# Routing and row sends of a mixture-of-experts layer moved from the opening into the main loop, with edge decays in four matmuls

## The chip, the cores and the metric

The kernel runs on one core of one Trainium2 chip. The metric is the time of one execution in microseconds on the device. All data are 32-bit floats.

## The reference, cut to what matters

Two layers work on 4096 tokens (8 sequences of 512) of 256 features. Each normalises its input and adds two branches to it.

The first layer's branches are a bidirectional Mamba-2 mixer and a top-1 mixture of eight experts:

```python
zxbcdt = u @ in_proj_w.T                      # z, xBC, dt
dt = softplus(dt + dt_bias)                   # 8 heads, both directions
xBC = silu(causal_conv(xBC, conv_w) + conv_b) # 4 taps
A = -exp(A_log)
# per chunk of 128 tokens, a = A*dt, A_cs = cumsum(a) in the chunk
Y_diag = einsum(C, B, exp(segsum(a)), x*dt)
Y_off  = einsum(C, state, exp(A_cs))          # exp(A_cs): the "edge decay"
y = Y_diag + Y_off + x*D ; gate with silu(z), normalise, @ out_proj_w.T

probs = softmax(xt @ Wr + br); gate = max(probs); idx = argmax(probs)
h1 = relu(xt @ W1[idx] + b1[idx]);  y = (h1 @ W2[idx] + b2[idx]) * gate
```

The second layer's branches are latent attention with 16 heads and a top-2 mixture of seven experts with a fixed capacity. The change does not touch them.

## The kernel before, in words

**Opening.** For each of the 8 sequences the kernel normalises four tiles of 128 tokens (kept in `xn0`), transposes them on TensorE and projects them to 24 columns: 16 of `dt`, 8 of routing (`norm_and_project`, lines 143 and 148). Then `route()` computes on VectorE the softplus of `dt` (lines 372 to 386), the product `da` of `dt` and `A` (line 390), and the routing: softmax, first maximum, the rank of every token in its expert (two matmuls `both`, lines 204 and 205), the slot of every token in a list sorted by expert and padded to blocks of 128 (`slot0`, line 409), and the expert of every block (`w_idx`, line 418). It ends with 32 indirect DMAs issued by GpSimd, one per tile, that send the normalised rows to their slots in `xd0` (line 422). There are 39 blocks.

After `route()` comes the first sequence's projection and convolution (`x_part`, `skip`, `bc_part`), two `tokens` parts, and then:

- `decays()` makes sums of `da` within chunks, and their exponentials.
- `edges()` makes the edge decay of every token, head and direction: per sequence and direction four matmuls with 8 weight columns each (line 452), an exponential of 8 x 512 (line 457) into a tile `e8` of the tag `row`, and a DMA to `exd` in DRAM (line 458). Tiles of the tag `row` have eight buffers, which the convolution's `cv` and `th` and the token transposes' `xt` use too.

In this part the order of instructions on each engine is a planner's.

**Main loop.** 64 iterations, one per chunk (sequence, step, direction): iteration n issues the segment sums of chunk n+1 (`seg`, line 879), prepares chunk n+2 (`au` on GpSimd, line 864, and the broadcast load of edge decays `ex`, line 868), does the chunk's own products (`yd`, line 917; `yoff`, line 935; `sp`, line 943) and `weigh` of the next chunk (`mt`, line 911). Between these stand parts of the neighbouring sequences' projections (`others`). The order on every engine is as written (`tc.manual_schedule`).

Four times in each iteration, from iteration 2 on, `fill(1)` takes a piece from the generator `blocks()`, or, when that is at its end, from `late()`, which finishes sequences for the second layer. In the last eight iterations there are two more. `blocks()` has five pieces per block:

1. transposes of the block's rows (line 495), the copy `xdT` on ScalarE (line 497), and `fetch(j + 1)`: the rows of the next block by SyncE, its `w1`, `w2` and `b12` by three indirect DMAs of GpSimd (line 482)
2. and 3. the two halves of the first product (line 507), with the relu on ScalarE for the first half and on VectorE for the second
4. and 5. the two halves of the second product (line 520), the bias and the write to `yd0`.

The pool `e2` of the blocks is opened ahead of the loop in the place of `xn0` and of the routing's tiles, so its first loads wait for what still reads those.

Of the kernel before, what the change touches and what calls it, by code (L numbers as in the profile page):

```python
# [16 lines left out]
P = 128  # L17
# [3 lines left out]
TPB = S // P  # L21
# [35 lines left out]
def tile_kernel(ctx: ExitStack, tc: tile.TileContext, t, out: bass.AP):  # L57
# [48 lines left out]
    xtd = dram.tile([B, P, KC, S], FP, name="xtd", tag="xtd")  # L106
    exd = dram.tile([B, 2, NH, S], FP, name="exd", tag="exd")
    fdd = dram.tile([B, NH, S], FP, name="fdd", tag="fdd")
# [214 lines left out]
    dt = l0c.tile(D3, FP, name="dt", tag="dt")  # L323
    da = l0c.tile(D3, FP, name="da", tag="da")
    gate = ctile("gate", [P, NTILE])
# [5 lines left out]
    mid = l0c.tile([P, NTILE, NH], FP, name="mid", tag="mid")  # L331
    dec_all = l0c.tile(D3, FP, name="dec_all", tag="dec_all")

# [5 lines left out]

    def route():  # L340
        pool, big = r0p, r0b
        proj = big.tile([P, NTILE, 2 * NH + NE], FP, name="proj0", tag="proj0")
        xTs = {}
# [45 lines left out]
        V.tensor_scalar(ea, ea, -1.0, None, ALU.mult)  # L389
        V.tensor_tensor(da, dt, bc(ea, 1, D3), ALU.mult)  # L390


        _, pr = softmax_experts(big, proj[:, :, 2 * NH :], br)
        m, oh = first_max(big, pr, "a")
        V.tensor_copy(gate, m)
        rank, n = ranks(big, bank, oh, lambda shape: row("rk_b").rearrange("p (a b) -> p a b", a=2))
        over = big.tile([P, NE, NTILE], FP, name="over", tag="over")
# [5 lines left out]
        for e in range(1, NE):  # L403
            V.tensor_tensor(end[:, e : e + 1], end[:, e : e + 1], end[:, e - 1 : e], ALU.add)
        first = big.tile([P, NE], FP, name="first", tag="first")
        V.tensor_tensor(first, end, nb, ALU.subtract)
        V.tensor_scalar(first, first, float(P), None, ALU.mult)
        V.tensor_tensor(rank, rank, bc(first, 1, E3), ALU.add)
        V.tensor_copy(slot0, slots_of(big, oh, rank, "a"))


        B3 = [P, NBLK, NE - 1]
# [4 lines left out]
        V.tensor_scalar(be, be, float(P), pidx, ALU.mult, ALU.add)  # L417
        V.tensor_copy(w_idx, be)

        sent = []  # L420
        for i in range(NTILE):
            one = G.indirect_dma_start(
                out=xd0, out_offset=bass.IndirectOffsetOnAxis(ap=slot0[:, i : i + 1], axis=0),
                in_=xn[:, i, :], in_offset=None, bounds_check=NBLK * P - 1, oob_is_err=False,
            )
            for other in sent:
                tc.declare_no_dep(one.ins, other.ins, reason="rows go to slots of their own")
            sent.append(one)

    def decays():  # L430
        dp = bank("dp", [P, 2, NTILE * NH], 0)
        for d in range(2):
            T.matmul(
                dp[:, d, :].rearrange("p (t h) -> p t h", h=NH), LOW[d], da[:, :, d * NH : (d + 1) * NH],
                start=True, stop=True,
            )
        A.activation(dec_tok.rearrange("p d t h -> p d (t h)"), dp, AF.Exp)
        hs = bank("hs", [P, NTILE, NH], 1)
        for d in range(2):
            r = slice(d * HP2, (d + 1) * HP2)  # L440
            T.matmul(hs[r], LOW[d][r, r], da[r, :, d * NH : (d + 1) * NH], start=True, stop=True)
        V.tensor_copy(mid, hs)
        ta = bank("ta", [P, NTILE * 2 * NH], 0)
        T.matmul(ta, ones, da.rearrange(f2), start=True, stop=True)
        A.activation(dec_all.rearrange(f2), ta, AF.Exp)

    def edges():
        for b in range(B):
            for d in range(2):
                ct = bank("ct", [NH, S], 0)  # L450
                for c in range(TPB):
                    T.matmul(
                        ct[:, c * P : (c + 1) * P], da[:, b * TPB + c, d * NH : (d + 1) * NH], MSK[d],
                        start=True, stop=True,
                    )
                e8 = row("e8")
                A.activation(e8[:NH, :], ct, AF.Exp)
                Y.dma_start(out=exd[b, d], in_=e8[:NH, :])

    route()  # L460
    l1c = tl = w_r = rb = w_q = w_o = w_uk = w_uv = w_kv = band = slot1 = wsel = proj1 = vt0 = qk0 = r1b = noop = None
# [4 lines left out]
    with ExitStack() as es:  # L466
# [8 lines left out]

        def fetch(j):
            xd = e2.tile([P, DM], FP, name="xd", tag="xd", bufs=3)
            Y.dma_start(out=xd, in_=xd0[j * P : (j + 1) * P, :])
            got = [xd]
            for name, n, bufs in (("w1", KC * FF, 2), ("w2", FC * DM, 2), ("b12", FC + DM, 2)):  # L480
                w = e2.tile([P, n], FP, name=name, tag=name, bufs=bufs)
                G.indirect_dma_start(
                    out=w, out_offset=None, in_=t[name], bounds_check=NE * P - 1, oob_is_err=False,
                    in_offset=bass.IndirectOffsetOnAxis(ap=w_idx[:, j : j + 1], axis=0),
                )
                got.append(w)
            return got

        def blocks():
            got = fetch(0)  # L490
            for j in range(NBLK):
                xd, w1, w2, b12 = got
                tp = bank("xdT_ps", [P, DM], "e")
# [3 lines left out]
                A.copy(xdT, tp)  # L497
                if j + 1 < NBLK:
                    got = fetch(j + 1)
                yield  # L500
                hT = [e2.tile([P, FC // 2, P], FP, name="hT", tag="hT", bufs=2) for _ in range(2)]
                for half in range(2):
                    hp = bank("h_ps", [P, FC // 2, P], "e")
                    for i in range(FC // 2):
                        f = half * FC // 2 + i
                        for k in range(KC):
                            T.matmul(  # L507
                                hp[:, i, :], w1[:, k * FF + f * P : k * FF + (f + 1) * P],
                                xdT[:, k * P : (k + 1) * P], start=(k == 0), stop=(k == KC - 1),
                            )  # L510
                    for i in range(FC // 2):
                        f = half * FC // 2 + i
                        if half == 0:
                            A.activation(hT[half][:, i, :], hp[:, i, :], AF.Relu, bias=b12[:, f : f + 1])
                        else:
                            V.tensor_scalar(hT[half][:, i, :], hp[:, i, :], b12[:, f : f + 1], 0.0, ALU.add, ALU.max)
                    yield
                yp = bank("y_ps", [P, DM], "e")
                for f in range(FC):
                    T.matmul(  # L520
                        yp, hT[f // 4][:, f % 4, :], w2[:, f * DM : (f + 1) * DM], start=(f == 0), stop=(f == FC - 1)
                    )
                    if f == 3:
                        yield
                yo = e2.tile([P, DM], FP, name="yo", tag="yo")
# [325 lines left out]
        class Chunk:  # L851
# [9 lines left out]
            def prepare(self):  # L861
                d = self.d
                self.au = p1.tile(HH, FP, name="au", tag="au")
                G.tensor_tensor(self.au, bc(da[:, self.i, d * NH : (d + 1) * NH], 2, HH), bc(TRI[d], 1, HH), ALU.mult)  # L864
                if not self.first:
                    self.ex = p2.tile([P, HC, P], FP, name="ex", tag="ex", bufs=3)
                    for i in range(2):
                        Y.dma_start(
                            out=self.ex[HD * i : HD * (i + 1), :, :],
                            in_=bc(exd[self.b, d, i::2, self.cols], 0, [HD, HC, P]),  # L870
                        )
# [67 lines left out]
            def behind(self):  # L939
# [7 lines left out]
                else:  # L947
                    d = self.d
                    G.tensor_tensor(
                        heads(st), heads(st), bc(dec_all[:, self.i, d * NH : (d + 1) * NH], 2, HP), ALU.mult  # L950
                    )
# [39 lines left out]
        batch[1].load()  # L991
        r0.close()
        xs.close()
        e2 = es.enter_context(tc.tile_pool(name="e2", bufs=2, side="right"))

        with tc.manual_schedule(engines=ENGINES):
# [31 lines left out]

            rows, rest = blocks(), late()

# [5 lines left out]
            for n in range(N):  # L1036
# [6 lines left out]
                ahead = chunk[n + 1] if n + 1 < N else None  # L1043
                begun = n >= 2

# [8 lines left out]
                if n % 8 == 5 and next_:  # L1054
                    pending.append(beginning)
                if begun:
                    fill(1)
                if ahead:
# [4 lines left out]
                turn()  # L1063
                if begun:
                    fill(1)
                now.before()
                if ahead:
                    ahead.pairs(batch[ahead.b])
                if begun:
                    fill(1)  # L1070
                turn()
                now.behind()
                if ahead:
                    ahead.weigh()
                if begun:
                    fill(1)
                while work:
                    turn()
                if n >= N - 8:
                    fill(2)  # L1080
# [532 lines left out]
```

## Time and profile before

| | us |
|---|---|
| median of three runs | 2159.49 (2159.13 to 2172.04) |
| the profiled execution | 2153.93 |
| its span, first to last instruction | 2152.2 |
| TensorE busy | 1874.2 (87%) |
| VectorE busy | 1463.6 (68%) |
| ScalarE busy | 1187.6 (55%) |
| GpSimd busy | 636.4 (30%) |
| opening, to the first `yd` | 0 to 169.8 |
| first layer's main loop and its end | 169.8 to about 1121 |
| expert blocks in it | 182.7 to 907.2 |
| second layer | from there to the end |

The profile names the engines PE (TensorE), PEld (its weight loads), DVE (VectorE), ACT (ScalarE), POOL (GpSimd) and SP (SyncE); "L507" is line 507 of the kernel. A 32-bit matmul shows as two records, a transpose as one. Ends of matmuls are modelled, so consecutive records overlap a little: the spacing of starts tells more than the durations. The page's second part cuts the span in 40 slices of 53.8 us; each digit is a busy share in tenths, and PEclk is the clock granted to TensorE in tenths of full speed.

### The profile page before, as it was taken

How to read it: one execution, taken by the hardware profiler on the slowest of the kernel's cores; microseconds unless marked ns; L12 is line 12 of the kernel's file. 1: busy time of each engine (PE TensorE's matmuls, PEld its weight loads, DVE VectorE, ACT ScalarE, POOL GpSimd, SP SyncE). 2: the span in 40 equal slices, each digit the busy share in tenths (PEclk: the TensorE clock that was granted, in tenths of full speed). 3: DMA queues.
4: the chain of work that ended last, by engine and by line, in shares of the span. 5: the costliest groups of instructions: out<-in, count | busy, mean ns of one | idle time of the engine just before them, and what ended most of it. 6: DMA issues, size and time to landing. Idle time of an engine off the chain costs nothing. (4 is left out here: it accounts for less than half of the span.)

```text
span 2152.2 us, 33599 instructions
## 1 busy us (share of the span) xinstructions
PE 1874.2 (87%) x11792; PEld 1240.4 (58%) x11792; DVE 1463.6 (68%) x3328; ACT 1187.6 (55%) x2562; POOL 636.4 (30%) x592
## 2 busy tenths in 40 slices
PE   5649999999999999987867778999999999999785
PEld 5325666766766676644544444656666666666343
DVE  5745666767584666577648896766666676767795
ACT  2235453545444354545426676767677777777563
POOL 0075453646363454445410253000000000000452
PEclk9879999999999999988887788999999999999787
DMA  7134454646463464444523342121121212121354
GB/s 257 56 103 169 152 191 146 222 142 221 140 203 138 135 230 134 142 135 127 162 94 112 96 144 89 63 103 61 65 81 60 97 63 82 62 77 54 89 109 94
DMA packets 156361, 263.69 MB, mean 123 GB/s; under 512 B 25018, under 2 KB 112622, under 8 KB 144290
## 3 DMA queue, kind: packets, MB, share of 16 engines
q1 hardware_dynamic: 124544, 144.70, 21.2%
q0 software_dynamic: 22320, 107.55, 15.3%
q10 hardware_dynamic: 9330, 9.31, 1.3%
q8 instruction: 93, 1.52, 0.3%
q14 instruction: 74, 0.61, 0.1%
HBM read 193.44 MB, written 72.75 MB: 124 GB/s over the span
## 5 line engine op out<-in xcount | busy, mean ns | idle before, releaser
L1348 DVE TENSOR_SCALAR s<-s_ps 128x512 f32<-128x512 f32 x512 | 317.7, 683 | 235.8 <-PE s_ps L1343 185.9
L1358 ACT ACTIVATE s<-s,ng 128x512 f32<-128x512 f32 x512 | 354.2, 726 | 29.0 <-DVE ng L1354 22.2
L1365 PE MATMUL p_ps<-ident,s 128*128 128x128 f32 x2048 | 297.3, 289 | 71.0 <-ACT pT L1366 60.2
L1365 PEld LDWEIGHTS p_ps<-ident,s 128*128 128x128 f32 x2048 | 244.3, 147 | 155.9 <-ACT pT L1366 94.2
L1366 ACT COPY pT<-p_ps 128x512 f32<-128x512 f32 x512 | 278.9, 590 | 88.5 <-PE p_ps L1365 63.9
L1350 DVE CUSTOM_DVE_ANT_0 s<-s,band 128x512 f32<-128x512 f32 x512 | 322.5, 685 | 0.0
L1308 POOL DMA_INDIRECT yg<-yd,at x64 | 67.6, 1057 | 710.6 <-PE s_ps L1343 650.7
L688 PE MATMUL pj<-xT,w_in 128*128 128x512 f32 x384 | 197.5, 640 | 12.3 <-DVE cv L701 9.5
L1343 PE MATMUL s_ps<-kT,qT 16*128 16x512 f32 x1024 | 174.7, 698 | 17.5 <-DVE s L1348 10.9
L507 PEld LDWEIGHTS h_ps<-xdT,w 128*128 128x128 f32 x1248 | 153.9, 197 | 32.9 <-issue 19.0
L507 PE MATMUL h_ps<-xdT,w 128*128 128x128 f32 x1248 | 158.8, 282 | 10.3 <-ACT xdT L497 10.3
L864 POOL TENSOR_TENSOR au<-da,half 128x512 f32<-128x512 f32 x64 | 75.1, 1174 | 258.0 <-PE seg L879 162.4
L701 DVE SCALAR_TENSOR_TENSOR cv<-pj,w_conv_w,cv 128x511 f32<-128x511 f32 (+2 forms) x192 | 143.0, 746 | 9.8 <-issue 5.6
L520 PE MATMUL y_ps<-w,hT 128*128 128x256 f32 x624 | 148.2, 380 | 0.0
L1374 PE MATMUL o_ps<-pT,vt 128*32 128x256 f32 x2048 | 139.6, 415 | 0.0
L520 PEld LDWEIGHTS y_ps<-w,hT 128*128 128x128 f32 x624 | 115.9, 191 | 34.8 <-issue 19.4
L937 POOL TENSOR_TENSOR yT<-yT,ex 128x512 f32<-128x512 f32 (+1 forms) x48 | 59.9, 1248 | 255.7 <-DVE ex L936 193.6
L1200 PE MATMUL e_hp<-e_xdT,e_w 128*128 128x256 f32 x448 | 121.7, 394 | 3.0 <-ACT e_xdT L1194 2.0
L688 PEld LDWEIGHTS pj<-xT,w_in 128*128 128x128 f32 x384 | 70.6, 201 | 91.9 <-issue 82.5
L926 DVE TENSOR_TENSOR yT<-yT,yd 128x512 f32<-128x512 f32 (+1 forms) x64 | 43.8, 684 | 116.4 <-PE yd L917 114.3
L1213 PE MATMUL e_yp<-e_w,e_hT 128*128 128x256 f32 x448 | 120.0, 390 | 0.2
L1374 PEld LDWEIGHTS o_ps<-pT,vt 128*32 128x32 f32 x2048 | 64.5, 118 | 80.0 <-issue 51.1
(275 smaller groups left out, 3133.1 us busy)
## 6 DMA issues: line engine op xcount, KB each, us to landing
ex<-exd SPq DMA_DIRECT2D x96, 128.0 KB
u<-in_u_dram SPq DMA_DIRECT2D x16, 512.0 KB
xtd<-xT SPq DMA_DIRECT2D x16, 512.0 KB
fr<-fdd SPq DMA_DIRECT2D x64, 128.0 KB
od<-os SPq DMA_DIRECT2D x32, 256.0 KB
xT<-xtd SPq DMA_DIRECT2D x15, 512.0 KB
e_w<-in_ei_dram SPq DMA_DIRECT2D x7, 1024.0 KB
e_w<-in_eo_dram SPq DMA_DIRECT2D x7, 1024.0 KB
```

The lines of the kernel that those rows point to most:

```text
L507: T.matmul(hp[:, i, :], w1[:, k * FF + f * P : k * FF + (f + 1) * P], xdT[:, k * P : (k + 1) * P], start=(k == 0), stop=(k == KC - 1),)
L520: T.matmul(yp, hT[f // 4][:, f % 4, :], w2[:, f * DM : (f + 1) * DM], start=(f == 0), stop=(f == FC - 1))
L688: T.matmul(pj, w_in[:, k, o * P : (o + 1) * P], self.xT[:, k, :], start=(k == 0), stop=(k == KC - 1))
L701: V.scalar_tensor_tensor(cv[:, s:], pj[:, : S - s], conv_w[:, q, 3 - s : 4 - s], cv[:, s:], ALU.mult, ALU.add)
L1200: T.matmul(hp, w1[:, k, f * P : (f + 1) * P], xdT[:, k, :], start=(k == 0), stop=(k == KC - 1))
L1343: T.matmul(sp[i], self.q[r, cols], self.k[r, :], start=True, stop=True)
L1348: V.tensor_scalar(self.p[i], sp[i], -CLAMP, CLAMP, ALU.max, ALU.min)
L1350: V.tensor_tensor_reduce(out=self.p[i], in0=self.p[i], in1=band[:, at : at + S], scale=1.0, scalar=-3.0e38, op0=ALU.mult, op1=ALU.max, acc ...
L1358: A.activation(self.p[i], self.p[i], AF.Exp, bias=self.ng[:, i : i + 1])
L1365: T.transpose(pp[:, k, :], self.p[i][:, k * P : (k + 1) * P], ident)
L1366: A.copy(pT[i][:, :, cc * P : (cc + 1) * P], pp)
L1374: T.matmul(op[32 * i : 32 * i + 32, half * 2 * P : (half + 1) * 2 * P], self.v[:, k, h * (AD + 1) : h * (AD + 1) + 32], pT[i][:, k, :], st ...
```

## The change

The edge decays of all sequences come from four matmuls. Each takes as its 128 weight columns the 8 heads of 16 tiles in one direction, for which `da` gets the direction as its outer axis. One exponential and one DMA follow, and `exd` is laid out by these groups. Half of the blocks' machinery is cut anew: the routing and the sends are a generator, `route0()`, of 22 pieces (six of arithmetic, 16 of two sends each), which stands ahead of `blocks()` in the row of fill pieces; the pool `e2` is opened when the first block begins; the rows of a block are transposed between the first and the second product of the block before, and its weights are fetched by name where their buffers come free. Fills begin with iteration 0, and the first two iterations of each sequence have one more. The second layer is as before.

```diff
-    exd = dram.tile([B, 2, NH, S], FP, name="exd", tag="exd")
+    exd = dram.tile([4, P, P], FP, name="exd", tag="exd")
+    EDGE = P // NH
...
-        V.tensor_tensor(da, dt, bc(ea, 1, D3), ALU.mult)
+        for d in range(2):
+            of = slice(d * NH, (d + 1) * NH)
+            V.tensor_tensor(da[:, d], dt[:, :, of], bc(ea[:, of], 1, [P, NTILE, NH]), ALU.mult)
+
+    def route0():
+        big = r0b
         _, pr = softmax_experts(big, proj[:, :, 2 * NH :], br)
+        yield
         m, oh = first_max(big, pr, "a")
         V.tensor_copy(gate, m)
+        yield
...
         V.tensor_copy(slot0, slots_of(big, oh, rank, "a"))
+        yield
...
         V.tensor_copy(w_idx, be)
+        yield
...
             sent.append(one)
+            if i % 2:
+                yield
...
     def edges():
-        for b in range(B):
-            for d in range(2):
-                ct = bank("ct", [NH, S], 0)
-                for c in range(TPB):
-                    T.matmul(
-                        ct[:, c * P : (c + 1) * P], da[:, b * TPB + c, d * NH : (d + 1) * NH], MSK[d],
-                        start=True, stop=True,
-                    )
-                e8 = row("e8")
-                A.activation(e8[:NH, :], ct, AF.Exp)
-                Y.dma_start(out=exd[b, d], in_=e8[:NH, :])
+        ct = bank("ct", [P, 4, P], 0)
+        for d in range(2):
+            for g in range(2):
+                T.matmul(
+                    ct[:, 2 * d + g, :], da[:, d, EDGE * g : EDGE * (g + 1), :].rearrange("p t e -> p (t e)"), MSK[d],
+                    start=True, stop=True,
+                )
+        e8 = row("e8").rearrange("p (g l) -> p g l", l=P)
+        A.activation(e8, ct, AF.Exp)
+        Y.dma_start(out=exd.rearrange("g p l -> p g l"), in_=e8)
...
-        def fetch(j):
-            xd = e2.tile([P, DM], FP, name="xd", tag="xd", bufs=3)
-            Y.dma_start(out=xd, in_=xd0[j * P : (j + 1) * P, :])
-            got = [xd]
-            for name, n, bufs in (("w1", KC * FF, 2), ("w2", FC * DM, 2), ("b12", FC + DM, 2)):
...
+        def fetch(j, *names):
+            if j < NBLK:
+                for name in names:
+                    n, bufs = {"xd": (DM, 3), "w1": (KC * FF, 2), "w2": (FC * DM, 2), "b12": (FC + DM, 2)}[name]
+                    w = held[name, j] = e2.tile([P, n], FP, name=name, tag=name, bufs=bufs)
+                    if name == "xd":
+                        Y.dma_start(out=w, in_=xd0[j * P : (j + 1) * P, :])
+                    else:
+                        G.indirect_dma_start(
...
         def blocks():
-            got = fetch(0)
-            for j in range(NBLK):
-                xd, w1, w2, b12 = got
+            nonlocal e2
+            r0.close()
+            xs.close()
+            e2 = es.enter_context(tc.tile_pool(name="e2", bufs=2, side="right"))
+            def turned(j):
+                xd = held.pop(("xd", j))
                 tp = bank("xdT_ps", [P, DM], "e")
                 for k in range(KC):
                     T.transpose(tp[:, k * P : (k + 1) * P], xd[:, k * P : (k + 1) * P], ident)
                 xdT = e2.tile([P, DM], FP, name="xdT", tag="xdT", bufs=3)
                 A.copy(xdT, tp)
-                if j + 1 < NBLK:
-                    got = fetch(j + 1)
-                yield
+                fetch(j + 2, "xd")
+                return xdT
+
+            fetch(0, "xd", "w1", "b12", "w2")
+            fetch(1, "xd", "w1", "b12", "w2")
+            yield
+            nxt = turned(0)
+            yield
+            for j in range(NBLK):
+                xdT, (w1, w2, b12) = nxt, (held.pop((name, j)) for name in ("w1", "w2", "b12"))
...
+                    if half == 0 and j:
+                        fetch(j + 1, "b12", "w2")
+                    yield
+                if j + 1 < NBLK:
+                    nxt = turned(j + 1)
                     yield
                 yp = bank("y_ps", [P, DM], "e")
...
                     if f == 3:
+                        fetch(j + 2, "w1")
                         yield
...
-        r0.close()
-        xs.close()
-        e2 = es.enter_context(tc.tile_pool(name="e2", bufs=2, side="right"))
+        e2 = None
...
-            rows, rest = blocks(), late()
+            rows, rest = itertools.chain(route0(), blocks()), late()
...
-                begun = n >= 2
...
-                if begun:
-                    fill(1)
+                fill(1)
...
                 while work:
                     turn()
+                if n % 8 < 2:
+                    fill(1)
```

The softplus part of `route()` stays where it was, under the name `steps()`. The other edits follow the new layouts of `da` and `exd`.

## The prediction

> **What bounds the kernel now.** I read the page first, then the busy time by stretch, then who waited for whom in the stretch of the change, then the timelines of GpSimd and TensorE there.
>
> ```profile
> PE 1874.2 (87%) x11792; PEld 1240.4 (58%) x11792; DVE 1463.6 (68%) x3328; ACT 1187.6 (55%) x2562; POOL 636.4 (30%) x592
> ...
> PE   5649999999999999987867778999999999999785
> ...
> PEclk9879999999999999988887788999999999999787
> ```
>
> TensorE is the fullest engine, and its row is full from slice 4 on: the first layer's main loop (about 170 to 1120 us) is bound by matmuls until the expert blocks end at 907. The holes are in slices 0 to 3, the opening. Columns of the next view: stretch, its length, busy us (and instructions) of each engine, granted TensorE clock, DMA share, GB/s.
>
> ```profile
> 137.00:170.00 33.00, 17.62 (x119) 11.59 (x119) 0.93 (x1) 8.10 (x16) 19.56 (x19) 0.66 0.22 68
> 170.00:191.00 21.00, 16.12 (x87) 8.29 (x84) 10.72 (x15) 13.50 (x40) 14.46 (x13) 0.92 0.38 126
> 191.00:235.00 44.00, 42.84 (x268) 30.55 (x267) 25.42 (x45) 19.74 (x55) 20.23 (x20) 1.00 0.63 217
> 235.00:900.00 665.00, 636.60 (x3805) 455.76 (x3805) 439.48 (x711) 311.18 (x856) 327.93 (x285) 0.98 0.51 172
> ```
>
> From 137 to 170 VectorE does one instruction. TensorE's 17.6 us are edge decays at a low clock. From 191 on TensorE is 96% busy. The waits name the cause of the hole (engine, line, awaited: total us, times, longest):
>
> ```profile
> ACT e L457 <- POOL xdt L774: 17.1, 2, 14.7
> ...
> PE ct L452 <- ACT e L457: 15.4, 2, 14.3
> ```
>
> An edge row `e8` needs a `row` buffer, which `xt` holds until GpSimd has made `xdt`; and GpSimd is sending rows:
>
> ```profile
> 130.08 2.21 POOL L422 DMA_INDIRECT xd<-xn,slot  x1 [0.30 <-issue]
> ...
> 151.92 0.98 POOL L422 DMA_INDIRECT xd<-xn,slot  x1 [0.30 <-issue]
> 153.21 0.98 POOL L422 DMA_INDIRECT xd<-xn,slot  x1 [0.30 <-issue]
> 154.20 1.06 POOL L864 TENSOR_TENSOR au<-da,half 128x512 f32<-128x512 f32 x1
> 155.20 2.04 POOL L774 TENSOR_TENSOR xdt<-xt,dt 128x512 f32<-128x512 f32 x2
> ```
>
> The 32 sends hold GpSimd from 108.6 to 154.2; then `xdt`, the rest of the edges, and iteration 0's `yd`, ready since `mt` at 137.9, starts at 169.76. TensorE's timeline gives the marks that I use:
>
> ```profile
> 169.76 1.10 PE L917 MATMUL yd<-mt,xdt 128*64 128x128 f32 x16
> ...
> 190.97 1.95 PE L507 MATMUL h_ps<-xdT,w 128*128 128x128 f32 x16
> ...
> 234.45 1.05 PE L935 MATMUL yoff<-bc,st 128*128 128x128 f32 x8
> ```
>
> **A. The opening.** Routing leaves it (all but three VectorE instructions), 32 sends leave, 64 edge matmuls (128 records) become 4, 16 exponentials and 16 writes become one each (0.6 us; one 256 KB write). The changed order interleaves softplus with `x_part`'s taps. With start-to-start times of the same instructions (tap 0.66, `x` 0.60, the softplus pair 0.60+0.34): the softplus is at 81.5 when the taps join it; 7 pairs 6.6 + 12 taps 7.9 + 4 `x` 2.4 + the end 2.2 = 19.1, so `da` is ready at 100.6, 3.4 later than now, but with all of `x` done (99.3, now 112.5). `skip` follows: fp 2.1, copy 0.6, fs 1.0, fd 0.7: 103.9, then the `bc` projection and its copy: the first `bc` tap at about 106. VectorE then has 12 taps, 4 `bc`, 12 of `yT`, `mid`, `cbm`, `mt`: 19.7, so `mt` is done and `yd` starts at 125.5: **44 us earlier**. The edge matmuls (4 x 0.5) lie inside. The `ex` loads still read 512-byte rows, on the same queue, and are wanted two iterations on; cost nothing, covered by those iterations.
>
> **B. Routing, now in iteration 0.** From `mt` to `slot0` VectorE has 11.6 us of routing instructions (summed from the groups of that stretch), its own add, `cbm` and `mt` 2.2, and the trip to TensorE for `both` about 1.2: 15, so `slot0` at 140.5. Queued behind on VectorE is iteration 1's `mt`, which feeds the second `yd`; it is late by some 8 us, but GpSimd is later still.
>
> **C. Sends, in iterations 1 to 4,** eight each. The page cannot show them there, so I bound them. Low: the 0.98 + 0.30 of an idle VectorE. High: 2.35, the longest, + 0.30. Nearest row: weight gathers in the full loop from 260 to 900 take 1.16 in the mean, at a similar VectorE load; I take 1.16 + 0.30 = 1.46. In the same queue lie 3 `au` (1.20), 3 `yT` (1.23), 4 `xdd` (1.10), 3 `st` (1.09), 15.0 by the same view. Sum 46.7 + 15.0 = 61.7: the last send at 202.2. These iterations are thus GpSimd's, 15.4 us each, against 7 us of TensorE without blocks (iteration 1 today, 174.6 to 181.6).
>
> Here a rule speaks against the change. The row: 20 sends beside a busy VectorE (108 to 138) took 1.22 in the mean, the last 12, beside an idle one, 0.98. The Trainium skill's page "SBUF — State Buffer" (section on the "DVE blocks DMA" trap) says that a GpSimd-issued DMA waits for descriptors while VectorE holds the shared port, about 620 ns becoming 3100. By that ratio a send costs 0.98 x 5 = 4.9 us, the sends 166 us and the change loses about 100; by the row 47. The row decides: the lock is taken by some instructions only.
>
> **D. First block.** Its weights reuse the memory of `xn0`, so gathers wait for the last send to land: 2 us (as the `fdd` write before its read, 116.06 to 117.99), issue 1.1, landing at most 5.3 (now 185.2 to 190.5): first `h_ps` at 210.6, in iteration 5 after `yoff` and `cb`. Today TensorE passes that place at 235.7, with blocks 0, 1 and most of 2 done: 3 transposes 1.1 + 3 h products 3.9 + 2.5 y products 3.8 = 22.3, less one transpose done ahead: 21.9. So the changed kernel is 25.1 ahead in time and 21.9 behind in work: **gain 3**. The loop is TensorE's, so deferred work is paid in full. Behind the six gathers (8.5 us) on GpSimd stand iteration 5's `yT` and `st`, done near 216; VectorE's `st` add and the `mt` after it wait for that, and the second `yd` from there, while TensorE has block 0's h product, two projections and a `seg`, some 10 us, so no new hole. The fallen clock costs about 2 of it (after the present hole 8 edge records take 1.87 instead of 1.04). Left: 1.
>
> **E. Rows transposed a product ahead.** This group of the loop (190 to 900) shows the wait:
>
> ```profile
> L507 PE MATMUL h_ps<-xdT,w 128*128 128x128 f32 x1248 | 158.8, 282 | 10.3 <-ACT xdT L497 10.3
> ```
>
> With the transposes ahead of a whole y product (3.8 us), the 0.4 us copy hides: **10.3 go**, and with them some clock: 0.98 over 665 us is 13 lost, of which I give 2.5. Next late are `cv`, `mt`, `z`, which stay. The y product now needs its PSUM buffer back from the second relu; one piece still lies between, and `y_ps` waits 0.0 today. Weight fetches are the same count in the same queue, spread by need. Without this cover (transposes right ahead of the h product) the 10.3 are back.
>
> **F. Pieces.** 22 routing + 196 block pieces in 256 + 16 + 16 fills, against 195 in 248 + 16: the blocks end in iteration 50 in both, and 70 instead of 69 fills are left for the late part. Nothing.
>
> **Sum:** 1 + 12.8 = about 14 off. The profiled execution took 2153.93 (span 2152.2): 2140 on its scale; the shown runs' median is 5.6 higher, so **2145.5**.
>
> **Rivals.**
> - *Pace by iteration* (0.25): if iterations keep their present 14.8 us (from 235 inside iteration 5 to 907, the last `y_ps`, at the end of iteration 50) whether they carry 0.80 or 0.86 of a block, the 21.9 of deferred work vanishes in slack. For: 28 us of idle and 13 of lost clock from 235 to 900. Against: 96% busy. Then 25 + 13: 2121.
> - *Waits move* (0.15): what waited for `xdT` waits for `cv`, `mt` or `z` instead. For: these are in-order and tight. Against: each is under 9 us today. Then about 2158.
> - *Sends choke* (0.10), the slower side: a send beside VectorE costs what the worst of today's cost. At 2.65 each GpSimd takes 84.8 + 15, first `h_ps` at 248.7, a loss of 35 less 13: 2181. It decides from 1.9 us a send, where D's loss eats E's gain. For: four of the 20 sends beside VectorE took 1.59 to 2.35. Against: the mean.
>
> **How the numbers follow.** The likeliest case (0.50) has its own range of 2128 to 2162, from the bounds of C (0.98 to 1.6 a send), A (4 either way) and E (5 to 15). About 1% (21.6 us) is what a measurement of this kernel can tell from no change. Faster by more: the pace rival and 0.3 of the likeliest case, 0.40; slower by more: most of the choking, 0.07; between: 0.53. The range, 2116 to 2168, leaves out the choking and the tail of the pace rival.
>
> **What would show it.** First `yd` at 121 to 130 and no wait on `xdt` by `e8` (A); `slot0` near 140 (B); sends spread over about 60 us at 1.1 to 1.3 each, GpSimd full there and TensorE half empty at a low clock (C); first `h_ps` at 203 to 219 (D); no wait of `h_ps` on `xdT` (E); last block ending near 893. It is wrong if the first `h_ps` comes after 225, or if the loop from iteration 5 to the last block runs at another pace than now per TensorE work.

## The result, and the profile after

The changed kernel takes **2131.86 us** in the median of four runs (2128.53 to 2141.17); the kernel before, run beside it on the same chip, 2159.8 (2159.13 to 2172.04). The ratio is **0.9863, with a 95% interval of 0.9829 to 0.9897**. It moved 27.9 us, where the forecast was 14.0 on the same scale: 2131.86 lies within the range of 2116 to 2168 and within the likeliest case's own range of 2128 to 2162, but it is faster by over 1%, which had a chance of 0.40 against 0.53 for "within 1%". The profiled execution took 2129.08, with a span of 2127.2 (2152.2 before: 25.0 less). The account by stage below is of these 25; the other 3 come from the two profiled executions, which lie 5.9 and 2.8 below the medians of their kernels.

The page of the changed kernel first: busy time by engine, then TensorE's row and its granted clock in 40 slices (53.2 us each).

```profile
PE 1861.6 (88%) x11672; PEld 1231.4 (58%) x11672; DVE 1461.2 (69%) x3329; ACT 1179.0 (55%) x2545; POOL 643.6 (30%) x592
...
PE   5666999999999999986758788999999999999785
...
PEclk9877999999999999997858778999999999999787
```

TensorE's row of before began 5, 6, 4, 9: a hole in slice 2, and full from slice 3 on. Now it begins 5, 6, 6, 6, 9: slice 2 is fuller, but slice 3 (160 to 213 us) has become thin, and its clock with it. The hole is not gone; it has become shallower and longer. The busy time by stretch shows the same in us (stretch, length, busy us and instructions of TensorE, its weight loads, VectorE, ScalarE and GpSimd, granted clock, DMA share, GB/s):

```profile
140.00:170.00 30.00, 19.60 (x74) 9.26 (x72) 20.06 (x45) 12.15 (x30) 19.21 (x18) 0.83 0.16 55
170.00:191.00 21.00, 10.49 (x52) 6.34 (x52) 11.34 (x16) 6.54 (x21) 17.86 (x18) 0.73 0.36 122
```

From 137 to 170 VectorE used to do one instruction; from 140 to 170 it now does 45. From 170 to 191 TensorE is half empty (10.5 of 21) where it was three quarters full, at a clock of 0.73 where it was 0.92. GpSimd's timeline gives the start and the end of the sends (start, duration, line, operation, and in brackets the idle time ahead of it):

```profile
148.53 1.22 POOL L441 DMA_INDIRECT xd<-xn,slot  x1 [7.06 <-DVE slot L426]
...
203.45 1.22 POOL L441 DMA_INDIRECT xd<-xn,slot  x1 [0.30 <-issue]
...
206.99 1.07 POOL L506 DMA_INDIRECT w<-in_w_dram,w_idx  x1 [1.24 <-DMA xd<-xn,slot]
```

GpSimd takes 56.1 us from the first send to the end of the last (148.53 to 204.67), with no gap over 0.31, the issue of a send. The first weight gather waits for the last send to land, as it was priced, and TensorE's timeline has the marks that follow:

```profile
130.38 1.98 PE L958 MATMUL yd<-mt,xdt 128*64 128x128 f32 x16 [4.18 <-DVE mt L952]
...
174.49 1.98 PE L958 MATMUL yd<-mt,xdt 128*64 128x128 f32 x16 [6.97 <-DVE mt L952]
...
212.84 2.02 PE L541 MATMUL h_ps<-xdT,w 128*128 128x128 f32 x16 [1.55 <-DMA w<-in_w_dram,w_idx]
```

`yd` of the first iteration starts 39.4 us earlier than before. The later ones wait for `mt` again and again. The waits from 108 to 235 (engine, line, awaited: total us, times, longest) sum that up and show a second wait linked to it:

```profile
PE yd L958 <- DVE mt L952: 27.5, 6, 7.0
...
DVE st L993 <- POOL st L990: 16.0, 3, 6.8
```

`mt` stands on VectorE behind the addition to `st`, and that waits for GpSimd's `st`, which stands behind sends. So the thin iterations 1 to 4 run in a ring: `yd`, a projection, `yoff`, VectorE's `ex`, GpSimd's `yT`, `xdd` and `st`, VectorE's `st`, `mt`, the next `yd`, some 14.7 us a round (174.49 to 189.21 to 203.87 for the `yd` of iterations 3, 4 and 5).

In the loop, the wait that the prediction removed is gone; what is left in front of the first product is the first block's weights:

```profile
L541 PE MATMUL h_ps<-xdT,w 128*128 128x128 f32 x1248 | 153.7, 277 | 1.6 <-DMA w<-in_w_dram,w_idx 1.6
```

**Where the 25 us went.** I cut both spans at the same place of iteration 5 (behind its `cb`), at the same place of iteration 50 (behind its `sp` and all block work) and at the end of the first layer, and read the busy time of each stretch. The second cut needs care. In the kernel before, the last `y_ps` ends at 907.24, ahead of that iteration's last projection and `sp` (2.7 us); in the changed kernel it stands one fill later, behind them, and ends at 883.37. So the cut of the kernel before is at 909.90, and the late parts then hold 794 records of TensorE each. Before:

```profile
235.70:909.90 674.20, 645.80 (x3847) 461.70 (x3847) 444.33 (x722) 312.79 (x859) 331.20 (x288) 0.98 0.51 170
909.90:1120.64 210.74, 162.25 (x794) 101.91 (x794) 145.63 (x298) 96.61 (x214) 89.79 (x81) 0.84 0.42 130
```

After:

```profile
212.84:883.37 670.53, 657.86 (x3986) 475.27 (x3986) 440.67 (x734) 319.75 (x875) 345.57 (x296) 0.99 0.57 182
883.37:1091.91 208.54, 158.39 (x794) 100.00 (x794) 141.89 (x297) 92.54 (x210) 89.98 (x81) 0.85 0.43 132
```

| stage | before | after | gain | forecast |
|---|---|---|---|---|
| to the place in iteration 5 | 235.7 | 212.8, with 21.9 us of block work still to do | 1.0 | 1 |
| from there to the end of block work | 674.2 | 670.5, with these 21.9 in it | 25.6 | 12.8 |
| late part of the first layer | 210.7 | 208.5 | 2.2 | 0 |
| second layer | 1031.6 | 1035.3 | -3.7 | 0 |

The second row holds the miss. The loop takes 3.7 us less than before and carries all 39 blocks in it instead of some 36 and a half. TensorE's idle time in it fell from 28.4 to 12.7 us, by 15.7. The remaining 9.9 are busy time: 657.9 us where 645.8 and the 21.9 make 667.7, at a granted clock of 0.99 instead of 0.98. About 1 of it is in the 21.9 itself, a sum of record durations that overlap; by the spacing of starts the same work took about 21.

### The profile page after: what moved, and what is told of

It is laid out like the page before. It is cut to its first block, busy times and chain, and to the rows that moved or that the text cites. A ratio compares the mean times of both kernels' runs of the same rounds, so it can differ in the third digit from the quotient of the medians.

```text
span 2127.2 us, 33330 instructions
## 1 busy us (share of the span) xinstructions
PE 1861.6 (88%) x11672; PEld 1231.4 (58%) x11672; DVE 1461.2 (69%) x3329; ACT 1179.0 (55%) x2545; POOL 643.6 (30%) x592
## 5 line engine op out<-in xcount | busy, mean ns | idle before, releaser
L728 PE MATMUL pj<-xT,w_in 128*128 128x512 f32 x384 | 204.5, 660 | 16.0 <-DVE cv L741 14.2
L541 PE MATMUL h_ps<-xdT,w 128*128 128x128 f32 x1248 | 153.7, 277 | 1.6 <-DMA w<-in_w_dram,w_idx 1.6
L933 ACT ACTIVATE mt<-seg,mid 64x64 f32<-64x64 f32 x512 | 109.9, 310 | 0.8
```

What stands on the lines that cost most here:

```text
L541: T.matmul(hp[:, i, :], w1[:, k * FF + f * P : k * FF + (f + 1) * P], xdT[:, k * P : (k + 1) * P], start=(k == 0), stop=(k == KC - 1),)
L728: T.matmul(pj, w_in[:, k, o * P : (o + 1) * P], self.xT[:, k, :], start=(k == 0), stop=(k == KC - 1))
```

## Experiments

The kernels ran on three chips (numbers 7, 0 and 1 below). The second layer, whose code is the same in all of them, takes 999 to 1006 us on chip 7, 1032 to 1035 on chip 0 (1024.5 in the kernel that leaves sends out) and 1042 to 1049 on chip 1. So ratios are always to the kernel before on the same chip (2119.79, 2156.19 and 2162.66 us in the median), and the stages of the first layer are compared by their own times. The changed kernel did not run on chip 7, so the four kernels there have it beside them only from other chips. The table gathers the marks of the profiled executions in us; "loop" is from the first `h_ps` to the end of the last `y_ps`, and "late part" from there to the end of the first layer. In the kernel before and in `only_edges` the last `y_ps` stands 2.7 us of work earlier, as said above, so their loops are shorter and their late parts longer by that much than those of the others.

| kernel | chip | ratio and 95% interval | first `yd` | first `h_ps` | loop | late part | end of first layer |
|---|---|---|---|---|---|---|---|
| before (`before_again`) | 0 | (one run) | 168.3 | 190.6 | 717.1 | 214.3 | 1122.0 |
| changed (`changed_again`) | 0 | 0.9876 (0.9849 to 0.9902) | 131.9 | 214.7 | 671.4 | 208.0 | 1094.0 |
| changed (`changed_third`) | 1 | 0.9906 (0.987 to 0.9942) | 131.8 | 214.5 | 674.5 | 211.3 | 1100.3 |
| `transposes_back` | 7 | 0.9965 (0.9948 to 0.9982) | 131.4 | 213.9 | 684.1 | 208.5 | 1106.5 |
| `transposes_back_2` | 1 | 0.9947 (0.9931 to 0.9963) | 131.0 | 213.5 | 684.2 | 211.8 | 1109.5 |
| `old_edges` | 7 | 0.9976 (0.9962 to 0.9989) | 141.8 | 226.5 | 669.8 | 211.6 | 1107.9 |
| `only_edges` | 0 | 0.9944 (0.9924 to 0.9963) | 157.5 | 185.2 | 712.8 | 207.5 | 1105.5 |
| `route_in_opening` | 7 | 0.9934 (0.9915 to 0.9953) | 158.2 | 187.5 | 695.2 | 220.7 | 1103.4 |
| `half_sends_early` | 7 | 0.9947 (0.993 to 0.9964) | 141.3 | 181.3 | 681.3 | 246.0 | 1108.7 |
| `half_the_sends` | 0 | 0.9842 (0.9808 to 0.9877) | 131.6 | 208.9 | 669.7 | 211.4 | 1090.0 |
| `early_even` | 1 | 0.9913 (0.9881 to 0.9945) | 141.9 | 180.1 | 699.2 | 218.2 | 1097.6 |
| `early_even_swap` | 1 | 0.9916 (0.9886 to 0.9947) | 142.3 | 181.7 | 695.9 | 217.6 | 1095.2 |

### The two kernels again

> The kernel before, for a profile on the same chip as the others. Theory and rival both: a first layer ending (last op matmul) at 1116 to 1121 as in the first profile, and a second layer of about 1001 to 1005 us as in the four runs; if the theory of the chip is wrong, the first layer itself is shorter here, with h_ps waiting less than 10.3 us on xdT.

> The changed kernel itself, beside the kernel before, on the chip of this group. The four runs so far stand beside a kernel before of 2119.8, not 2159.8, so this chip's second layer is some 30 us faster and the change may be worth less here. Theory (transposes 15 to 23, edges 10 to 15, as from the two runs that undo them, 2113.9 and 2114.8): 2095 to 2103, ratio to before 0.988 to 0.992. Rival (part of the 28 us of the first pair belonged to a difference between executions, not to the change): 2106 to 2112, ratio 0.994 to 0.997, and undoing either part costs only 3 to 6.

> The changed kernel, for comparison with the other three on this chip. Ratio to the kernel before 0.983 to 0.990; first yd at 131, first h_ps at 213 to 215, first layer's last operation at 1092 to 1094.

The changed kernel ran on two of the three chips, at 2127.9 (2124.8 to 2130.7) and 2143.59 (2132.3 to 2150.2). The three intervals of its ratio overlap, and the marks of its opening repeat within 2 us. The first layer's end does not: 1091.9 at first, then 1094.0 and 1100.3.

### The transposes back ahead of their own product

```diff
             for j in range(NBLK):
-                xdT, (w1, w2, b12) = nxt, (held.pop((name, j)) for name in ("w1", "w2", "b12"))
+                xdT = turned(j)
+                yield
+                w1, w2, b12 = (held.pop((name, j)) for name in ("w1", "w2", "b12"))
...
-                if j + 1 < NBLK:
-                    nxt = turned(j + 1)
-                    yield
                 yp = bank("y_ps", [P, DM], "e")
```

> The changed kernel with one part undone: a block's rows are transposed right ahead of its own first product again, as before the change; routing pieces, sends, edges and fetches by name stay. Theory (the loop's gain of about 23 us, where the prediction had 12.8, comes from the transposes standing a product ahead): h_ps waits on xdT again, 8 to 15 us in all, the granted clock between 235 and 900 falls from 0.99 to 0.98, and the time is 15 to 23 us above the changed kernel's 2131.9, so 2147 to 2155. Rival (denser pieces, 0.86 instead of 0.80 of a block an iteration, fill slack that the loop had anyway): within 5 us of 2131.9 although h_ps waits again.

> The changed kernel with each block's four transposes back right ahead of its own first product, beside the changed kernel itself on the same chip. Theory (the transposes are worth the wait they removed and a little clock): 12 to 13 us more than the changed kernel, all of it in the 39 blocks of the first layer; the first h_ps at the same place, within 1 us. Rival (the loop's whole gain of 22.9 us over the kernel before is the transposes'): 20 us or more. Rival (the deferred block work vanishes in slack whatever the transposes do, and they are worth little): under 5 us.

The second run has the changed kernel beside it on chip 1. The group of the first product, and the busy time from the first `h_ps` to the last `y_ps`, with the transposes back (`transposes_back_2`):

```profile
L541 PE MATMUL h_ps<-xdT,w 128*128 128x128 f32 x1248 | 156.5, 280 | 14.5 <-ACT xdT L524 11.6 <-DMA w<-in_w_dram,w_idx 2.9
```

```profile
213.46:897.69 684.23, 661.54 (x3986) 477.11 (x3986) 443.99 (x732) 319.10 (x875) 339.79 (x296) 0.99 0.55 179
```

And in the changed kernel on the same chip (`changed_third`):

```profile
214.46:888.99 674.53, 660.58 (x3986) 476.99 (x3986) 439.74 (x732) 319.63 (x875) 343.84 (x296) 0.99 0.56 181
```

The wait on the copy comes back with 11.6 us, and the loop takes **9.7 us** more: 8.7 as TensorE's idle time (22.7 against 13.9, to rounding) and 1.0 as busy time. The first layer ends 9.2 later, and the medians differ by 7.2 (2150.75 against 2143.59, their ratios' intervals overlapping). On chip 7 the loop had 684.1, which is 12.7 more than the changed kernel on chip 0. So the transposes are worth 10 to 13 us, not 20, and not under 5.

The same run tells where the rest of the loop's 25.6 is. It has the transposes of the kernel before, with nearly the same wait (11.6 here, 10.3 there), and the deferred work of the changed kernel. Were the deferred work paid in full, its loop would take 674.2 + 21.9 = 696.1; it takes 684.2, **11.9 less**. TensorE's idle time is 5.7 lower than in the kernel before (22.7 against 28.4), most of it in the waits of `bp` for VectorE's `z` (4.9 instead of 8.5) and of `yd` for `mt` (hardly any instead of 2.0); its busy time is 661.5 instead of 645.8 + 21.9 = 667.7. The run also keeps the new order of weight fetches. No run took that apart; no wait of a product on a block's weights stood in the loop before.

### The edges: undone, and alone

`old_edges` is the changed kernel with the 64 matmuls, 16 exponentials and 16 writes; `only_edges` is the kernel before with the four matmuls and nothing else. The core of both is this exchange in `edges()`, made backwards in the one and forwards in the other:

```diff
-        for b in range(B):
-            for d in range(2):
-                ct = bank("ct", [NH, S], 0)
-                for c in range(TPB):
...
-                e8 = row("e8")
+        ct = bank("ct", [P, 4, P], 0)
+        for d in range(2):
+            for g in range(2):
...
+        e8 = row("e8").rearrange("p (g l) -> p g l", l=P)
```

> The changed kernel with the edge decays as before: 64 matmuls of 8 weight columns, 16 exponentials, 16 writes, all ahead of the first yd on TensorE. Theory (with the sends gone from the opening, the edges still cost their own time there): 16 exponentials about 0.9 apart stand ahead of the first yd, which comes 10 to 15 us later than in the changed kernel (130.4), and the first h_ps as much later; time 2142 to 2147. Rival (the hole was all the wait on xdt; once GpSimd is free the edges hide beside VectorE's chain): first yd within 3 us of 130.4, time within 5 us of 2131.9.

> The kernel before with one part of the change alone: edge decays in four matmuls (with the layouts of da and exd); routing, sends and transposes as before. Theory (the first yd is held by xdt behind the sends in any case, so the edges alone bring only the part after xdt): first yd at 157 to 160 instead of 169.8, time 8 to 12 below before. Rival (edges were the hole): first yd near 140, 25 or more below before.

Without the new edges the first `yd` of the changed kernel comes at 141.8, ten later, and the first `h_ps` at 226.5, twelve later; the first layer ends at 1107.9 instead of 1092 to 1100. The loop takes 669.8, as in the changed kernel. The waits of `old_edges` from 108 to 200 show the way of these ten us: the token transposes come late behind the edge matmuls, and GpSimd's `xdt` waits for them.

```profile
POOL xdt L813 <- ACT xt L810: 14.4, 3, 10.1
```

Alone, the new edges take 14.7 us off the median (2141.53 against 2156.19) and 16.5 off the first layer's end. They do not open the hole fully: the first `yd` then waits for GpSimd, which is still sending rows.

```profile
PE yd L921 <- POOL xdt L777: 18.8, 1, 18.8
```

The edge matmuls alone thus bring about half of the 28 us. 10.8 us of the 16.5 are there at the first `yd`; 5.4 of these are lost again until the first `h_ps` (27.7 us after `yd` instead of 22.3), and 4.3 come from the loop and 6.8 from the late part. For the last of these no cause was found.

### Routing and sends: all in the opening, half in the opening

`route_in_opening` runs `route0()` to its end behind `steps()`, and fills begin in iteration 2 as they used to. `half_sends_early` puts the arithmetic and 16 sends there.

```diff
     steps()
+    for _ in route0():
+        pass
...
-            rows, rest = itertools.chain(route0(), blocks()), late()
+            rows, rest = blocks(), late()
```

> The changed kernel with routing and all 32 sends back in the opening (and fills from iteration 2 as before); edges in four matmuls and transposes a product ahead stay. Theory (pieces of routing and sends bring nothing by themselves: the head start of 40 us is paid back because the first block begins in iteration 5 instead of 2): first yd near 157, held by xdt behind the sends; first h_ps 178 to 183 in iteration 2, worth 200 to 205 at the place where the changed kernel has 212.8; time 2119 to 2127, so faster than the changed kernel. Rival (taking the sends out of the opening is what brings the gain): 2145 or more.

> The changed kernel with the routing arithmetic and 16 of the 32 sends put back into the opening, where GpSimd has nothing else to do between slot0 and xdt; the other 16 stay as pieces, so that the first block begins in iteration 2. Theory (what sets the first block is GpSimd's queue, and half of it fits into an idle gap): first yd near 138, first h_ps 175 to 182 in iteration 2; 10 to 16 us below the changed kernel, 2116 to 2122. Rival (VectorE sets the opening: 11.6 us of routing ahead of mt cost what the earlier sends bring): 2128 to 2135.

With everything in the opening the first `yd` waits 18.8 us for `xdt` again and starts at 158.2, 27 later than in the changed kernel, but the blocks start 27 earlier (187.5), in iteration 2. The first layer ends 3 to 12 us later (1103.4 against 1092 to 1100). Where the routing stands thus matters far less than the 27 us by which it moves the first `yd`: what the opening gains, the thin iterations 1 to 4 give back for the most part, as D's sum says.

`half_sends_early` starts its blocks at 181.3 and ends them at 862.7, but in iteration 47 instead of 50, and its late part grows to 246 us (the view begins 1.5 us behind the last `y_ps`):

```profile
864.20:1108.70 244.50, 183.74 (x912) 113.91 (x910) 157.82 (x322) 111.90 (x259) 99.90 (x93) 0.83 0.38 118
```

TensorE is busy for 75% of it. The 16 iterations without block work are not short (15.4 us each, with the end of the layer in it); they only run emptier. To have the blocks done early is worth nothing.

### Half of the sends left out

This kernel leaves every second send out, so half of the rows never reach their slots; it shows the time without 16 sends.

```diff
         for i in range(NTILE):
+            if i % 2:
+                yield
+                continue
```

> The changed kernel with every second send left out (half of the rows never reach their slots), to price the sends; all pieces stay, one send each. Theory (GpSimd's queue of sends sets iterations 1 to 4 and the first block): the first h_ps comes 16 x 1.3 = 21 us earlier, at 190 to 194, and the time falls by 15 to 21 against the changed kernel on this chip. Rival (VectorE's and TensorE's own chain sets these iterations, about 11 us each): first h_ps only 8 to 12 earlier. A second rival (what is gained ahead of the blocks is lost after them, because iterations without block work are held by other waits): first h_ps 21 earlier, but under 8 us left at the end.

Sixteen sends at 1.3 us each are 21 us of GpSimd. The first `h_ps` comes only **5.8 us** earlier than in the changed kernel on the same chip (208.9 against 214.7), and the first layer ends 4.0 earlier. The waits of GpSimd from 145 to 205 show what takes the place of the sends:

```profile
POOL yT L979 <- issue: 7.4, 2, 4.2
...
POOL yT L979 <- DVE ex L978: 5.9, 1, 5.9
```

GpSimd now stands idle ahead of `yT`, waiting in part for VectorE's `ex`, which itself waits for TensorE. So the ring of small products, at a low clock (0.81 from 150 to 205 here, 0.80, 0.72 and 0.78 in three executions of the changed kernel), is nearly as slow as the sends. GpSimd paces iterations 1 to 4, but only by some 1.5 us each (5.8 over 4).

### Blocks earlier and evenly spread

`early_even` has the arithmetic and 16 sends in the opening, and no extra fill in the first two iterations of a sequence, so that the blocks end in iteration 50 as in the changed kernel. `early_even_swap` also issues `mt` ahead of the addition to `st`, which takes the wait for GpSimd out of the ring.

```diff
     steps()
+    routing = route0()
+    for _ in range(14):
+        next(routing)
...
-                if n % 8 < 2:
-                    fill(1)
```

```diff
-                now.behind()
                 if ahead:
                     ahead.weigh()
+                now.behind()
```

> The changed kernel with the routing's arithmetic and the first half of the sends in the opening, the other half as pieces from iteration 1, and blocks spread so that they end in iteration 50 as before. Theory (the first blocks can start two iterations sooner, and work brought forward is worth its time so long as blocks cover the whole loop): first h_ps near 182, the last y_ps near 876, first layer's end near 1083, some 11 us less than the changed kernel. Rival (the opening gives back what it gains: first yd comes 10 later, and the loop has no slack left to take in): within 4 us of the changed kernel. Rival (the late part grows again as it did with blocks ending at iteration 47): slower than the changed kernel.

> The kernel of early_even with VectorE's weighing of the next step (mt) issued ahead of the addition to the state that waits for GpSimd. Theory (in iterations without much block work the ring yd, ex, GpSimd's st, VectorE's st, mt, yd sets the pace, and the swap cuts it): the late part some 5 to 10 us shorter, the time up to 10 less than early_even. Rival (TensorE has enough queued wherever blocks run, so that the wait is covered): within 3 us of early_even.

Both are no better than the changed kernel on that chip: 2143.93 and 2142.74 against 2143.59. The first block starts 34 us earlier, yet the loop ends only 9.7 earlier (879.3 against 889.0), and the first layer 2.7. The first part is lost in the opening and in TensorE's own queue, which stands at the first block's transposes until rows have been sent and read back, as the timeline of `early_even` shows:

```profile
175.71 0.66 PE L525 MATMUL xdT_ps<-ident,xd 128*128 128x128 f32 x2 [9.63 <-DMA xd<-xd]
```

The second part is lost behind the loop: the late part takes 218.2 instead of 211.3. The swap moves the first layer's end by 2.4 us, and nothing that the times can tell.

## Why the prediction was right or wrong

**A, the opening: right in kind, 4.9 late.** The first `yd` came at 130.38, not 125.5. `da` was ready at 101.0 (100.6 in the sum) and the first `bc` tap started at 106.68 (106), so 3.9 of the slip lie in the last list of VectorE, 19.7 us in the sum and 23.6 measured. Its last instructions were stretched, by 3.0 together; VectorE's timeline of the changed kernel, the last `yT` and `mt` of iteration 0, and `mt` of iterations 2 and 3:

```profile
123.83 2.98 DVE L798 SCALAR_TENSOR_TENSOR yT<-x,w_d_rep,yT 128x511 f32<-128x511 f32 x2
...
126.94 1.32 DVE L798 SCALAR_TENSOR_TENSOR yT<-x,w_d_rep,yT 128x511 f32<-128x511 f32 x1
128.18 2.06 DVE L952 TENSOR_TENSOR mt<-mt,cbm 128x1024 f32<-128x1024 f32 x1
...
155.98 1.22 DVE L952 TENSOR_TENSOR mt<-mt,cbm 128x1024 f32<-128x1024 f32 x1
...
173.22 1.22 DVE L952 TENSOR_TENSOR mt<-mt,cbm 128x1024 f32<-128x1024 f32 x1
```

And GpSimd's beside them:

```profile
123.31 2.95 POOL L814 TENSOR_TENSOR xdt<-xt,dt 128x512 f32<-128x512 f32 x2 [3.72 <-ACT xt L811]
...
127.67 5.65 POOL L814 TENSOR_TENSOR xdt<-xt,dt 128x512 f32<-128x512 f32 x4
...
156.28 1.77 POOL L441 DMA_INDIRECT xd<-xn,slot  x1 [0.30 <-issue]
...
174.07 1.22 POOL L441 DMA_INDIRECT xd<-xn,slot  x1 [0.31 <-issue]
```

Before, `xdt` ran while VectorE had nothing to do (1.02 each); now the two meet, and both slow down: `xdt` to 1.4 to 1.5, `mt` from 1.22 to 2.06, `yT` from 0.74 to 1.3 or 1.5. The sum took VectorE's durations from a stretch without that company.

**B, routing in iteration 0: 7.6 late.** `slot0` was written at 148.05 instead of 140.5: 4.9 are A's, and the way from `yd` took 17.7 instead of 15. Iteration 1's `mt` (1.2) went in between, not behind as the sum had it, and two copies of VectorE took 1.02 each where the same copies had taken 0.17 and 0.22 in the kernel before. One ran beside GpSimd's `xdt`, the other beside its `au`, and each ended within 0.1 us of it.

**C, the sends: the outcome right, the reason half right.** A send took 1.04 in the mean (1.16 in the sum), and from the first to the end of the last GpSimd needed 56.1 us, not 61.7; that made good most of B's delay, and the last send ended at 204.67 (202.2). "These iterations are thus GpSimd's" is half of the truth: without every second send they are only 5.8 us shorter, since the ring of in-order waits is nearly as long. *Sends choke* is out: beside a VectorE that was busy for half of the time (25.6 of 55 us from 150 to 205), no send took over 1.77, where the estimate from the ratio in the Trainium skill's page "SBUF — State Buffer" (the "DVE blocks DMA" trap) was 4.9. This does not refute the page: its ratio is for a DMA beside a `tensor_copy` of VectorE, and no copy ran beside a send from 150 to 205. Nor is the mean of 1.04 a price for any half-busy neighbour. What counted was which instruction ran: the four sends that began inside an `mt` took 1.77 once and 1.22 three times and ended 0.85 us after it (two of them are shown under A), the first send took 1.22 in every execution, and all others 0.98 to 1.08, beside the taps `cv` too. The four of 1.59 to 2.35 in the kernel before also ran beside `yT`, `bc` and `mt`, so the row's 1.22 was the mean of two kinds. That iterations 1 to 4 give VectorE mostly taps was not in the argument, and was lucky.

**D, the first block: right to 2 us, by errors that cancel.** `h_ps` at 212.84 (210.6): A and B were 7.6 late together, and the sends 5.6 shorter. That is 22.9 earlier in time and 21.9 behind in work. But the sentence **"the loop is TensorE's, so deferred work is paid in full" failed**, and it is the step that made the forecast too cautious. With the old transposes put back, the loop took in the 21.9 us of deferred work for about 10.0 (684.2 - 674.2): 5.7 went into TensorE's idle time, about 1 was the sum's (overlapping records), and some 5 was busy time that the same work no longer took, at a clock of 0.99 instead of 0.98. A TensorE at 96% of its time in records had still some room. It is what the prediction named as a sign of being wrong: the loop from iteration 5 to the last block ran at another pace per TensorE work, and the blocks ended at 883.4 instead of 893. This compares single executions on two chips; the loop of the changed kernel alone differs by 4.0 between three of them, so the 11.9 are good to about that.

**E, the transposes: right.** 12.8 was forecast, of which 10.3 as the wait and 2.5 as clock; undoing them costs 9.7 on the same chip (8.7 idle, 1.0 busy), 12.7 across chips. The wait is 0 in the loop. What became late next did not take its place: *Waits move* is out, with 12.7 us of idle left in the whole loop.

**The loop's 25.6** is therefore 9.7 from the transposes and 11.9 from deferred work that was not paid; 4.0 more is the difference between two executions of the changed kernel (670.5 and 674.5; the third has 671.4), which is not settled. *Pace by iteration* was half right: it had all of the 21.9 vanish, and 2121; the measured time lies midway between it and the forecast.

**F, the pieces: right on the blocks' end, and nearly on the late part.** The blocks end in iteration 50, as forecast, if one fill later. The late part became 2.2 shorter, which the sum had at nothing. Cut at the same place, it is 205 to 212 in ten executions whose blocks end in iteration 50, 205 already with only the edges changed, 211 in the kernel before and in the changed kernel on chip 1; it is 218 to 221 in the three kernels with routing in the opening and without the extra fills. What makes it vary has not been found; TensorE waits in it mostly for the late pieces' `xn` on VectorE (28.6 us before, 30.6 after).

The two misses were of the same sign: 12.8 in the loop and 2.2 behind it, less 3.7 that the second layer, unchanged, took more in that execution.

## What to carry to other kernels

Work that is moved into a later loop need not be paid at the loop's mean price, even where the bounding engine shows 96%: look at the loop's idle time and clock first. Here about half of it was free. In the other direction, time gained ahead of a loop is worth little if the iterations after it then run thin on a ring of in-order waits: shifting the first `yd` by 27 us or the first block by 34 moved the end of the layer by 3 to 12. Before pricing instructions that are pulled forward, look at who will then run beside them: durations taken from a stretch in which the neighbour was idle were 0.6 to 0.75 too short for a `yT` and 0.8 for `mt`. And when two executions are cut "at the last" of something, check that the same work lies on both sides of the cut.

## What the runs showed of the hardware

- VectorE and GpSimd slowed each other in some elementwise work: `mt` took 1.22 alone and 2.06 beside `xdt`; `xdt` 1.02 alone and 1.4 to 1.5 beside `yT` and `mt`. The taps `cv`, which read a projection's result from PSUM, did not slow: three took 2.31 beside an `au` of 1.06 (174.96 to 177.27). Two small copies of VectorE took 1.02 beside GpSimd's products, 0.17 and 0.22 without.
- An indirect send of GpSimd took 0.98 beside an idle VectorE and up to 1.08 beside taps. The four that began inside an `mt` took 1.22 to 1.77, in each of three executions, and ended 0.85 us after it.
- The same second layer takes 999 to 1006, 1032 to 1035 (1024.5 in the kernel without half of its sends) and 1042 to 1049 us on three chips, with mean granted clocks of 0.929 to 0.935, 0.915 to 0.919 and 0.903 to 0.915 over it. So a difference of 30 us between whole kernels on different chips says nothing here.
- In the thin iterations 1 to 4 the granted clock falls to 0.72 to 0.80 (150 to 205), and some projections `pj` of four matmuls take 3.5 to 3.8 us instead of 1.9 (two to four of seven); so a hole filled with sparse work stays expensive for the work in it.
